# Softmax reciprocals of the first attention pass computed and fetched about one unit earlier

## The chip, the cores and the metric

The kernel runs on one core of one Trainium2 chip, in one launch. The metric is the device time of one execution in microseconds (us); lower is better. All data are 32-bit floats.

## The reference, cut to what matters

The input is 8 images of 32x32 positions with 512 channels. Two layers follow each other. Layer 0 is group norm, self-attention with 8 heads of 64 channels over the 1024 positions of an image, and a residual:

```
x_norm = group_norm(x)
q, k, v = split(x_norm @ w_qkv + b_qkv)          # 8 heads of 64
weight  = softmax((q * scale) @ (k * scale)^T)   # 1024 x 1024 for each head
out     = (weight @ v) @ w_out + b_out
x       = x + out
```

Layer 1 is a deformable attention: a layer norm and a projection, a depthwise 7x7 convolution with stride 2 that yields 256 sample points an image, keys and values from bilinear samples at these points, attention of all 1024 positions to the 256 samples, and a small MLP with residual. The change touches layer 0 alone, and in it the division by the softmax's sums.

## The kernel before, in words

The work of layer 0 (the first pass) is a row of 256 units, one after the other. A unit is one pair of heads and one tile of 128 queries of one image: 32 units an image (4 head pairs times 8 query tiles), 8 images. Four units in a row make a block of 512 queries for one head pair; there are 64 blocks, counted here from 0, so an image has eight.

The program of each engine is in the order in which the Python code issues it (`InOrder`). Work that belongs to other units is put in between by hand: `at(place, step)` files a step under a place on the axis of units, and `run_due(until)` issues all filed steps with a smaller place, in the order of their places. `push` for unit n issues, in this order:

- `scores`: 8 score matmuls on TensorE (two heads, 128 queries, 1024 keys), the negated row maximum on VectorE (`nmax`), the exponential on ScalarE (`e`), which also accumulates each row's sum in `sums`;
- all steps due before n + 0.8 (`before`);
- the transposes of `e` into `sq` on VectorE, in 32x32 squares;
- in odd units, `moved`: 16 copies that carry two units' squares from `sq` to `et`, which completes the transpose. They are issued on SyncE's queue (SP in the profile), which takes its instructions strictly in order;
- all steps due before n + 1 (`after`).

After an odd unit u, `attention_out` files the products with v under n = u + 3: `part` at n + 0.02 and n + 1.02, 16 matmuls each, which add up a block's output in the one PSUM tile `av` (`ps_av` has a single buffer). When u is the last unit of a block it also files the division:

- `share` (VectorE, then SP): the reciprocal of the block's sums into `rs`, a 32x32 transpose into `rsT`, and a DMA of 16 KB to a DRAM tile, `rs_d`;
- `spread` (SP): two DMAs that read `rs_d` back, each replicated over 64 partitions, into the tile `inv`. `inv` has one buffer in this pass (`n_inv` is 1), and these DMAs wait for the landing of `rs_d`;
- `scale` at n + 1.85 (VectorE): `attT` = `av` times `inv`. After it the next block may write `av`.

Other DMAs that SP carries in this pass, all in program order with those above: the results `mid` and `hat_d` of the image before, placed near the ends of units, and the operands `hat_x` of a convolution that is computed early beside the attention. Loads of x and of weights are issued by GpSimd (POOL), which also adds the convolution's taps and does part of the norms.

Of the kernel before, what the change touches and what calls it, by code (L numbers as in the profile page):

```python
# [240 lines left out]
def attention_then_deformable_attention(  # L241
# [115 lines left out]
    def at(place, step):  # L357
        due.append((place, len(due), step))
# [37 lines left out]
    with ExitStack() as l0:  # L396
# [54 lines left out]
        att = MovedAttention(nc, ident, ps_mm, ps_sc, ps_av, work, dram, 1)  # L451
# [181 lines left out]
        def attention_out(attT, hp, qt, n, et, sums, room):  # L633

            blk, t = divmod(qt, NQT)
            half = t // 2
            at(n + 0.02, lambda: att.part(et, room["v"], half, True))
            at(n + 1.02, lambda: att.part(et, room["v"], half, False))
            if half == 0:
                return  # L640

            share = {}

            def scale():
                t = attT[hp, blk] = work.tile([P, QB], F32, tag="attT", name="attT", bufs=NQB * NHP)
                att.scale(t, share["inv"])

            at(n - 1.1, lambda: att.share(sums))
            at(n - 0.1, lambda: share.update(inv=att.spread()))
            at(n + 1.85, scale)  # L650

        def last_places(n, t):
# [114 lines left out]
        for b in range(B):  # L767
# [20 lines left out]
            for hp in range(NHP):  # L788
                for qt in range(NT):
                    n = first + hp * NT + qt  # L790
                    if n % per == 0 and b > 0:
                        last, attT = attT, {}
                        out_steps(
                            b - 1, last,
                            [[n + p - 2.4, n + p - 1.4, n + p, int(n + p) + 0.85, n + p + 1.55]
                             for p in out_places],
                        )
                    t = qkv[b, hp]
                    et = att.push(
                        before=lambda n=n: run_due(n + 0.8),  # L800
                        after=lambda n=n: run_due(n + 1),
                        tiles=1,
                        at=qt % NQT,
                        q=t["q", qt // NQT][:, ts(qt % NQT, P)],
                        k=t["k"],
                    )
                    if et is not None:
                        attention_out(attT, hp, qt, n + 3, et, att.sums, t)
# [4 lines left out]
    with ExitStack() as l1:  # L813
# [56 lines left out]
        att = Attention(nc, ident, ps_mm, ps_sc, ps_av, work, dram, 2)  # L870
# [422 lines left out]
```

## Time and profile before

| | |
|---|---|
| three timed runs | 3562.83, 3573.17 and 3572.59 us; median 3572.59 us |
| profiled execution | 3563.64 us, of which the span of the core is 3561.9 us |
| first pass in the span | from the start to about 2240 us |
| busy over the span: PE / DVE / ACT / POOL | 3408.9 / 2527.3 / 1807.6 / 1538.3 us |
| `inv` reads: issues, time from issue to landing (min / median / max) | 256 in both passes, 3.3 / 4.4 / 9.1 us |

PE is the matmul engine TensorE, DVE is VectorE, ACT is ScalarE, SPq is SyncE's queue. Nearly all instructions go through one helper line, L54, so groups are told apart by the names of their tiles, output before input: `attT<-av,inv` is the step `scale`, `rsT<-rs` the transpose in `share`, `rs_d<-rsT` its DMA, `inv<-rs_d` the reads in `spread`, `et<-sq` the copies in `moved`. In a list of instructions the first column is the start and the second the duration, both in us; what stands in square brackets at the end of a row is the idle time of the engine just before it and what ended it. In a list of waits the three figures are the sum in us, how often, and the longest.

### The profile page before, as it was taken

What the parts mean: (1) busy time and instruction counts of PE and PEld (TensorE: products, weight loads), DVE (VectorE), ACT (ScalarE), POOL (GpSimd) and SP (SyncE); (2) the same over time, 40 slices, a digit from 0 to 9 for tenths busy, and PEclk for the clock granted to TensorE, in tenths of its full rate; (3) what the DMA queues carried; (4) which work ended last, traced back from release to release, by engine and by line L of the source; (5) the groups of instructions that cost most, each with busy time, mean ns of one, the idle gap of its engine ahead of it and who ended that gap; (6) DMA issues with size and microseconds to landing.
All of it is one profiled execution on the core that took longest, in us unless ns stands there. A gap on an engine that the chain in (4) does not pass through costs nothing.

```text
span 3561.9 us, 45200 instructions
## 1 busy us (share of the span) xinstructions
PE 3408.9 (96%) x14568; PEld 1686.4 (47%) x14568; DVE 2527.3 (71%) x3373; ACT 1807.6 (51%) x3919; POOL 1538.3 (43%) x1903
## 2 busy tenths in 40 slices
PE   7999999999999999999999998899998989899998
PEld 4444544554554454454454453444444444444443
DVE  4767778878878787788887876247767677665654
ACT  2343356566566566556566552135555455544442
POOL 1001216646735645654654653305444443542322
PEclk9999999999999999999999999899999999999999
DMA  4666657766766666666766766446556555555653
GB/s 141 167 162 174 195 157 193 209 164 177 218 160 172 201 175 186 196 184 168 205 180 167 205 175 187 155 136 201 190 174 196 167 191 171 187 195 188 223 185 126
DMA packets 446587, 641.64 MB, mean 180 GB/s; under 512 B 77104, under 2 KB 240944, under 8 KB 444304
## 3 DMA queue, kind: packets, MB, share of 16 engines
q1 hardware_dynamic: 415712, 536.67, 51.9%
q0 software_dynamic: 29488, 100.00, 9.4%
q8 instruction: 116, 1.90, 0.2%
q10 hardware_dynamic: 1152, 2.10, 0.2%
q14 instruction: 119, 0.97, 0.1%
HBM read 246.38 MB, written 123.73 MB: 104 GB/s over the span
## 4 chain that ended last, share of the span: by engine, by line
PE 75%; DVE 5%; SPq 5%; POOL 4%; ACT 4%; DMA 4%; issue 3%; POOLq 0%; DVEq 0%; ACTq 0%
PE mm L54 48%; PE sc L54 14%; PE av L54 13%; SPq L54 5%; ACT e L54 2%; DMA inv<-rs_d 1%; POOL chunk L54 1%; DVE sq L54 1%; DVE chunk L54 1%; POOL oa L54 1%; DVE nmax L54 1%; DMA et<-sq 1%; ACT L54 1%; POOL row L54 1%; DMA et<-sq_d 0%
## 5 line engine op out<-in xcount | busy, mean ns | idle before, releaser
L54 ACT ACTIVATE e<-sc,nmax 128x1024 f32<-128x1024 f32 (+1 forms) x1024 | 802.6, 797 | 627.9 <-DVE nmax L54 626.8
L54 DVE TENSOR_REDUCE nmax<-sc 128x1 f32<-128x1024 f32 (+1 forms) x640 | 750.6, 1214 | 351.3 <-PE sc L54 351.0
L54 DVE STREAM_TRANSPOSE sq<-e 128x1024 f32<-128x1024 f32 x640 | 764.6, 1225 | 253.2 <-ACT e L54 237.1
L54 POOL TENSOR_TENSOR oa<-part_x,oa 128x256 f32<-128x256 f32 x852 | 635.6, 746 | 590.4 <-ACT part_x L54 545.5
L54 ACT ACTIVATE part_x<-pad_x,dww_x 128x256 f32<-128x256 f32 x852 | 435.2, 541 | 241.8 <-POOL oa L54 239.4
L54 PE MATMUL sc<-k,q 64*128 64x512 f32 x2048 | 539.5, 619 | 18.8 <-ACT e L54 17.2
L54 PE MATMUL av<-et,v 128*64 128x256 f32 x4096 | 510.8, 393 | 33.4 <-DVE attT L54 18.5
L54 PE MATMUL mm<-xT,wqkv 128*128 128x512 f32 x1024 | 472.8, 606 | 3.1 <-issue 3.1
L54 PEld LDWEIGHTS av<-et,v 128*64 128x64 f32 x4096 | 277.1, 139 | 344.6 <-issue 156.7
L54 POOL TENSOR_TENSOR chunk<-parts,chunk 128x256 f32<-128x256 f32 x240 | 179.9, 750 | 388.7 <-ACT parts L54 375.2
L54 PEld LDWEIGHTS sc<-k,q 64*128 64x128 f32 x2048 | 187.3, 186 | 283.1 <-issue 190.6
L54 PEld LDWEIGHTS mm<-xT,wqkv 128*128 128x128 f32 x1024 | 187.9, 191 | 242.5 <-issue 236.8
L54 POOL TENSOR_TENSOR mv<-mv,minus_half 128x1 f32<-128x1 f32 x128 | 77.3, 604 | 509.5 <-DVE mv L54 508.2
L54 PEld LDWEIGHTS mm<-wqkv,xT 128*128 128x128 f32 x2048 | 234.7, 192 | 26.1 <-issue 26.1
L54 PE MATMUL mm<-wqkv,xT 128*128 128x128 f32 x2048 | 245.4, 278 | 0.0
L54 PE MATMUL mm<-wm,zT 128*128 128x512 f32 x512 | 238.4, 608 | 1.3 <-ACT zT L54 1.0
L54 PE MATMUL mm<-w,attT 128*128 128x512 f32 x512 | 235.5, 604 | 1.3 <-DVE attT L54 1.3
L54 PE MATMUL mm<-wo,attH 128*128 128x512 f32 x512 | 230.8, 593 | 0.4
L54 PE MATMUL mm<-hat_h,wqq 128*128 128x512 f32 x512 | 230.7, 593 | 0.0
L54 DVE SCALAR_TENSOR_TENSOR od<-pad_x,dww_x,od 128x256 f32<-128x256 f32 x276 | 216.9, 786 | 5.5
L54 ACT ACTIVATION_READ_ACCUMULATOR e<-sc,nmax 128x1 f32 x1024 | 209.4, 204 | 0.0
L54 PE MATMUL mm<-w,hat_x 128*128 128x512 f32 x384 | 172.7, 600 | 0.0
(163 smaller groups left out, 3565.3 us busy)
## 6 DMA issues: line engine op xcount, KB each, us to landing
et<-sq SPq DMA_DIRECT2D x2048, 128.0 KB, 2.8
sq_d<-sq SPq DMA_DIRECT2D x128, 512.0 KB, 4.4
et<-sq_d SPq DMA_DIRECT2D x128, 512.0 KB, 4.2
inv<-rs_d SPq DMA_DIRECT2D x256, 128.0 KB, 4.4
hat_h<-hat_d SPq DMA_DIRECT2D x16, 1024.0 KB, 7.9
xr<-mid SPq DMA_DIRECT2D x64, 256.0 KB, 5.4
x<-in_x_dram POOLq DMA_DIRECT2D x60, 256.0 KB, 4.0
out_dram<-res POOLq DMA_DIRECT2D x60, 256.0 KB, 3.3
```

Of the source, the lines that this page charges most:

```text
L54: return self.tc.keep_in_program_order(op(*args, **kwargs))
```

## The change

Two places change by hand, both in `attention_out`. With u for the last unit of the block (n = u + 3), `share` moves from u + 1.9 to u + 1.1 and `spread` from u + 2.9 to u + 1.9.

```
-            at(n - 1.1, lambda: att.share(sums))
-            at(n - 0.1, lambda: share.update(inv=att.spread()))
+            at(n - 1.9, lambda: att.share(sums))
+            at(n - 1.1, lambda: share.update(inv=att.spread()))
             at(n + 1.85, scale)
```

In the order of issue this means: `share` runs in the `before` part of unit u + 1 (ahead of that unit's transposes) where it ran in its `after` part; `spread` runs in the `after` part of unit u + 1, so ahead of the 16 copies of unit u + 2, where it ran behind them. The place of `scale`, the amount of work and all tiles stay as they were.

## The prediction

> **What bounds the kernel now.** I read the page's busy line first, then the list of waits, then the instructions around one wait, then windows with the granted clock.
>
> ```profile
> PE 3408.9 (96%) x14568; PEld 1686.4 (47%) x14568; DVE 2527.3 (71%) x3373; ACT 1807.6 (51%) x3919; POOL 1538.3 (43%) x1903
> ...
> PE 75%; DVE 5%; SPq 5%; POOL 4%; ACT 4%; DMA 4%; issue 3%; POOLq 0%; DVEq 0%; ACTq 0%
> ```
>
> TensorE carries the time. The second line is the chain that ended last: 14% of it lies on SPq, DMA and VectorE together, where PE stood waiting. A change that removes no matmul can gain only what PE waits. The list of waits says where:
>
> ```profile
> DVE attT L54 <- DMA inv<-rs_d: 66.4, 38, 5.4
> ...
> PE av L54 <- DVE attT L54: 18.5, 9, 3.3
> ...
> PE av L54 <- DMA et<-sq: 14.0, 3, 8.2
> ```
>
> VectorE's `scale` waited 38 times of 64 for the broadcast reciprocals. Nine times this reached PE, since the next block's first product may not write `av` before `scale` has read it: 18.5 us. The third row is put down to the copies, but is mostly the same wait. At 102.94 us the group of copies had landed at 99.83, and `attT` ended only at 102.9; the other two are taken up below. The wait at block 13, engine by engine (SP, DVE, PE):
>
> ```profile
> 490.88 0.33 SPq L54 DMA_DIRECT2D rs_d<-rsT  x1
> 497.21 11.16 SPq L54 DMA_DIRECT2D et<-sq  x16
> 508.42 1.27 SPq L54 DMA_DIRECT2D inv<-rs_d  x2
> ...
> 507.46 2.37 DVE L54 STREAM_TRANSPOSE sq<-e 128x1024 f32<-128x1024 f32 x2 [1.23 <-ACT e L54]
> 513.99 0.69 DVE L54 TENSOR_TENSOR attT<-av,inv 128x512 f32<-128x512 f32 x1 [4.16 <-DMA inv<-rs_d]
> ...
> 509.42 1.99 PE L54 MATMUL sc<-k,q 64*128 64x512 f32 x8
> 514.74 3.38 PE L54 MATMUL av<-et,v 128*64 128x256 f32 x16 [3.33 <-DVE attT L54]
> ```
>
> The reads of `inv` stood behind 16 copies in SP's order, though `rs_d` had landed 16 us earlier (492.29). They landed at 513.87; VectorE idled 4.16 us, PE 3.33 us. Of those 3.33 us the copies explain nothing: they had landed at 510.50. And the same 16 matmuls, 1.95 us elsewhere, took 3.38 us. The windows show why (first figure PE's busy time; the clock stands after POOL's):
>
> ```profile
> 511.40:514.70 3.30, 0.01 (x1) 0.00 (x0) 0.71 (x2) 0.00 (x0) 0.76 (x2) 0.93 0.87 216
> 514.70:517.70 3.00, 2.96 (x14) 1.71 (x16) 2.96 (x4) 0.94 (x1) 0.00 (x0) 0.50 0.95 308
> ```
>
> After the idle stretch the clock is at half for 3 us (back at 1.00 after 517.7): half of that is lost too.
>
> **Part 1: the waits that go.** `spread` now precedes the 16 copies. Its new landing is estimated for each block as the end of unit u's copies, plus that block's own landing times of `rs_d` and `inv`: it comes 6 to 25 us before `scale` could start, in every block but the last. (Block 63 stays: its `share` and `spread` are issued behind the same last copies as before.) So each `scale` runs when VectorE reaches it, and PE next waits for the later of its own work and the copies. The nine gaps are .36, .23, 3.33, 2.50, 3.04, 2.43, 3.29, 2.80 and .49 us, six of them the sixth block of an image (blocks 13 to 53). In those six the copies landed 0.9 to 1.7 us before PE would need them, so all 18.5 us go. The 2.7 us of block 0 go. At 2168.60 (block 61, gap 3.0) the copies landed only at 2165.90, and part 2 delays them by 0.8: 1.9 us go. At 2194.82 (block 62, gap 8.2) the copies landed at 2191.63: 3.1 us go and 5 us stay. Sum 18.5 + 2.7 + 1.9 + 3.1 = 26.2 us.
>
> The clock comes on top. The records show half clock after five of these gaps, at 514, 1068, 1347, 1900 and 2169 us, for 2.9, 5.9, 3.4, 2.9 and 3.4 us of matmuls: half of 18.5 is 9.3 us. Here the Trainium skill speaks otherwise: "TensorE: Matmul & The Clock Gate", Part 1, has the array fall to half clock after an idle window of about 3.4 us. The gaps here, 2.4 to 3.3 us, are shorter; by the rule none would cost clock, and the sum would be 26.2. The trace has half clock after five and none after those of 2.5 us at 791.83 and 3.29 us at 1624.95. I take the trace's 9.3. The dip at 2190 us I leave, as 5 us of its gap stay.
>
> I take off 2.5 us for the short gaps of the first image and of 2108, where PE elsewhere waits for exponentials (17 gaps, 17.2 us, `sc<-k,q` on `e`) and may give the time back. Net gain: 26.2 + 9.3 - 2.5 = 33.0 us.
>
> **Part 2: what moves on SP's queue.** Per block one `rs_d` issue (0.3 to 0.8 us) and two `inv` issues (1.27 us), no more than before. `rs_d` now issues right behind unit u's copies, ahead of `mid` and `hat_d` placed late in unit u + 1; these go later by the half microsecond of that issue, and wait for results of VectorE and POOL anyway. The new cost is that SP stands at `inv` until `rs_d` has landed, with the next 16 copies behind it.
>
> ```profile
> 612.89 14.06 SPq L54 DMA_DIRECT2D et<-sq  x16
> 627.05 0.54 SPq L54 DMA_DIRECT2D hat_d<-hat  x1
> 627.68 0.53 SPq L54 DMA_DIRECT2D mid<-xr  x1
> 628.30 0.58 SPq L54 DMA_DIRECT2D hat_d<-hat  x1
> 628.97 0.76 SPq L54 DMA_DIRECT2D rs_d<-rsT  x1
> 630.34 13.03 SPq L54 DMA_DIRECT2D et<-sq  x16
> ```
>
> This is the tightest kind: 3.4 us from one group of copies to the next. With `rs_d` at 627.05, its own landing of 3.6 us and 1.3 us for `inv`, the next copies start at about 632.0, 1.6 us late. They had landed 7.1 us before PE used them, and no `inv` follows them now. Over the blocks this room is 2.1 to 13 us, and `rs_d` landed in 1.4 to 7.6 us in this pass (median 2.4). Here a rule speaks against the change: "DMA: Bandwidth & Descriptors", Anatomy of one DMA, says that a wait on a semaphore is sat out by the issuing sequencer and that most of a fixed 2 us is the receipt from the target memory. With 2 us, 7 of 63 groups of copies start late, with the 3.6 us measured in this busy place 17, by up to about 3 us, and in both cases none later than PE needs it. I take 3.6 and 0 us.
>
> A second hold is none: `inv` has one buffer, but the previous `scale` ends about 13 us before the new issue (613.6 against about 630 above). POOL's queue gets nothing new and nothing on it is passed.
>
> **Part 3: VectorE.** Reciprocal 0.20 and transpose 0.21 us come 64 times, before and after. They now stand between `nmax` and `sq`, which delays unit u + 1's squares by 0.4 us; their copies go only with unit u + 2. The next `nmax` waits behind the same sum of work. Taken as 0; if the cover is gone in a quarter of the 17 gaps on `e`, 1.6 us, and if it were gone in all blocks, 64 times 0.41 = 26 us. The 66 us of VectorE's idle time at `scale` that vanish feed no other row: where PE did not wait, the next `nmax` waited for scores.
>
> **Rivals.**
> (a) *The next thing is late.* PE's wait at `attT` becomes one on the copies, which in the sixth blocks land only 0.9 to 1.7 us ahead. If they land 2 us later, the seven gaps keep about 1 us each and perhaps the clock dips: gain 33 - 7 - 7 = 19 us, 3554 us. Against it: in these blocks SP idles 6 us before that group, so it is not pushed.
> (b) *Nothing.* The reads land earlier but the matmuls after them wait for exponentials, or `inv` is held by something the trace does not show: 3562 to 3580 us. Against it: the gaps end within 0.1 us of `attT`.
> (c) *Slower: SP blocks on the landing of `rs_d`.* If behind 16 copies in flight `rs_d` needs L us, PE's new stall, summed over the groups' measured room, is 0 up to 3.65, 2.4 us at L = 5, 15.6 at 7, 41.9 at 9, 70.6 at 10. Against a gain of 33 it decides from about 8.6 us; at 9.5 it gives 3572.6 + 56 - 33 = 3596 us. For it: landings of 7.2 and 7.6 us exist. Against it: four fifths are below 3.7.
> That the change does not do what it says I exclude: the steps are filed when `push` of unit u has returned, and both places lie in unit u + 1.
>
> **The numbers.** The sum is made on the profiled execution: 3563.6 - 33.0 = 3530.6 us. The median of the runs is 9 us above that execution; from the median it is 3572.6 - 33.0 = 3539.6, and I give 3539. Chances: forecast 0.70, (a) 0.14, (b) 0.08, (c) 0.08. About 0.3%, 11 us, is what a measurement here can tell from no change. Faster by more 0.84, within 0.08, slower 0.08. The range reaches down to the profiled base with some 10 us of secondary gain (3521) and up through (a), to 3562.
>
> **What would show it.** Right: no row of `attT` waiting for `inv` over a few us in sum, PE's waits for `attT` near 0, the sixth blocks at full clock, `inv` issued ahead of each even group of copies and SP waiting there for `rs_d` 1 to 4 us. Wrong: new rows of `av` waiting for `et<-sq` well over 14 us, or landings of `rs_d` above 8 us. If the waits vanish and the time does not fall, look at `sc<-k,q` on `e`.

## The result and the profile after

| | before | after |
|---|---|---|
| timed runs (before: the three above and one more) | 3555.2 to 3573.2 us, median 3567.7 (4 runs) | 3522.9 to 3528.6 us, median 3526.4 (4 runs) |
| profiled execution / its span | 3563.64 / 3561.9 us | 3522.86 / 3521.2 us |
| the first pass ends (its last output product, `mm<-w,attT`, starts) at | 2234.1 us | 2199.2 us |

The changed kernel is faster: the ratio is 0.9888, with a 95% interval of 0.9858 to 0.9919, so 1.1% or about 41 us. The forecast was 3539 us in a range of 3521 to 3562.

The busy line and the chain of the page after:

```profile
PE 3388.6 (96%) x14568; PEld 1679.5 (48%) x14568; DVE 2534.7 (72%) x3373; ACT 1809.8 (51%) x3919; POOL 1536.3 (44%) x1903
...
PE 81%; POOL 4%; ACT 4%; DVE 4%; issue 3%; DMA 2%; SPq 2%; POOLq 0%; ACTq 0%; DVEq 0%
```

PE's share of the chain rose from 75% to 81%; SPq, DMA and VectorE gave up what it gained. PE is also busy 20 us less for the same matmuls, since more of them run at full clock: in these two profiles the granted clock is at half for 159 us in sum before and for 116 after, and half of the difference is 21 us. The list of waits after, for VectorE, PE and SP (us in sum, times, longest):

```profile
DVE attT L54 <- DMA inv<-rs_d: 2.1, 1, 2.1
...
PE av L54 <- DMA et<-sq: 13.0, 4, 6.5
...
SPq L54 <- DMA rs_d<-rsT: 108.3, 57, 6.4
```

`scale` waits for its reciprocals once (the last block), where it waited 38 times; PE has no row of `av` behind `attT` left. What came instead is on SP: it stands 57 times for the landing of `rs_d`, 108 us in sum. Block 13 again, by SP, DVE and PE:

```profile
485.21 0.53 SPq L54 DMA_DIRECT2D rs_d<-rsT  x1
487.48 1.27 SPq L54 DMA_DIRECT2D inv<-rs_d  x2
493.15 10.86 SPq L54 DMA_DIRECT2D et<-sq  x16
...
505.69 0.65 DVE L54 TENSOR_TENSOR attT<-av,inv 128x512 f32<-128x512 f32 x1
...
505.35 1.99 PE L54 MATMUL sc<-k,q 64*128 64x512 f32 x8
507.27 1.95 PE L54 MATMUL av<-et,v 128*64 128x256 f32 x16
```

The reads now issue 6 us ahead of the 16 copies, not behind them. `attT` starts when the transposes ahead of it on VectorE end, and the product follows the scores without a gap and takes 1.95 us, not 3.38. The window of that product has the clock at 1.00:

```profile
507.20:510.20 3.00, 3.00 (x21) 1.63 (x20) 2.97 (x5) 1.33 (x3) 1.01 (x2) 1.00 0.82 220
```

In the tightest kind of block (around 630 us before), SP's queue reads:

```profile
617.20 0.53 SPq L54 DMA_DIRECT2D hat_d<-hat  x1
617.83 0.43 SPq L54 DMA_DIRECT2D mid<-xr  x1
618.35 0.86 SPq L54 DMA_DIRECT2D rs_d<-rsT  x1
...
621.75 1.28 SPq L54 DMA_DIRECT2D inv<-rs_d  x2
623.13 13.48 SPq L54 DMA_DIRECT2D et<-sq  x16
```

The squares of the last group were ready at 621.04, so this group starts 2.1 us late (1.6 was estimated), and PE, which uses it at 643.3, does not notice. A row of `hat_d` and one of `mid` still stand ahead of `rs_d`: it passes only some of them, not all as the forecast had it.

**Where the time went.** The lead of the changed kernel is the start of the same product before minus after, in the first profiles of the two kernels. A block's gap at `attT` lies ahead of the next block's first product and is counted with the block whose `attT` it is.

| stage of the first pass | lead at its end, us | gained in it |
|---|---|---|
| up to block 12 | 3.8 | 3.8 |
| six sixth blocks (13 to 53), each with its clock stretch | | 5.1 + 2.9 + 6.3 + 4.7 + 3.7 + 4.6 = 27.3 |
| all other blocks up to 60 | 33.7 | 2.6 |
| blocks 61 to 63, up to the last output product | 34.8 | 1.1 |
| from there to the end of the program | 40.8 | 5.9 |

### The profile page after: what moved, and what is told of

It is laid out like the page before. It is cut to its first block, busy times and chain, and to the rows that moved or that the text cites. A ratio compares the mean times of both kernels' runs of the same rounds, so it can differ in the third digit from the quotient of the medians.

```text
span 3521.2 us, 45344 instructions
## 1 busy us (share of the span) xinstructions
PE 3388.6 (96%) x14568; PEld 1679.5 (48%) x14568; DVE 2534.7 (72%) x3373; ACT 1809.8 (51%) x3919; POOL 1536.3 (44%) x1903
## 4 chain that ended last, share of the span: by engine, by line
PE 81%; POOL 4%; ACT 4%; DVE 4%; issue 3%; DMA 2%; SPq 2%; POOLq 0%; ACTq 0%; DVEq 0%
PE mm L54 51%; PE sc L54 16%; PE av L54 15%; ACT e L54 2%; SPq L54 2%; POOL chunk L54 1%; POOL row L54 1%; DVE chunk L54 1%; ACT L54 1%; DVE nmax L54 1%; POOL oa L54 0%; DMA et<-sq_d 0%; DMA sq_d<-sq 0%; POOL rows L54 0%; POOL hat L54 0%
## 5 line engine op out<-in xcount | busy, mean ns | idle before, releaser
L54 PE MATMUL sc<-k,q 64*128 64x512 f32 x2048 | 536.6, 619 | 17.1 <-ACT e L54 15.4
L54 PE MATMUL av<-et,v 128*64 128x256 f32 x4096 | 503.5, 388 | 13.9 <-DMA et<-sq 13.0
L54 DVE SCALAR_TENSOR_TENSOR od<-pad_x,dww_x,od 128x256 f32<-128x256 f32 x276 | 226.4, 820 | 5.5
## 6 DMA issues: line engine op xcount, KB each, us to landing
et<-sq SPq DMA_DIRECT2D x2048, 128.0 KB
inv<-rs_d SPq DMA_DIRECT2D x256, 128.0 KB
```

What stands on the lines that cost most here:

```text
L54: return self.tc.keep_in_program_order(op(*args, **kwargs))
```

## The experiments

Two theories were to be told apart first. *Order on SP*: the time was lost because the reads stood behind 16 copies in SP's order. *VectorE's order*: the gain comes from the reciprocal moving away from in front of the next `nmax`. All edits are to the two places, or to the queue, of the first pass.

**The reciprocal alone moved.**

```
+            at(n - 1.9, lambda: att.share(sums))
             at(n - 0.1, lambda: share.update(inv=att.spread()))
```

> Only the reciprocal and its DMA move (u + 1.1); the broadcast reads stay behind the 16 copies at u + 2.9. Theory (the reads' place in SP's order is what cost): the 38 waits of attT for inv stay near 66 us, PE's gaps at attT stay near 18 us, and the time is that of before within 0.3% (3557 to 3578). Rival (VectorE's order, the reciprocal out of the way of the next nmax): the gain comes here, 3525 to 3540.

Measured: 3568.7 us, ratio to before 0.9997 (0.9983 to 1.0011). Its waits of VectorE, and of PE:

```profile
DVE attT L54 <- DMA inv<-rs_d: 69.1, 34, 7.5
...
PE av L54 <- DVE attT L54: 19.5, 8, 3.6
```

All the waits are still there. The VectorE theory falls.

**The reads alone moved.**

```
             at(n - 1.1, lambda: att.share(sums))
+            at(n - 1.05, lambda: share.update(inv=att.spread()))
```

> Only the reads move: the reciprocal stays at u + 1.9 and the reads follow it at u + 1.95, ahead of the copies of u + 2. Theory: the waits of attT for inv vanish and most of the gain comes (3525 to 3545), but SP stands longer for the landing of rs_d, 130 to 200 us in sum instead of 108, and some groups of copies come later than with the full change, which may cost it 0 to 10 us. Rival (VectorE's order): no gain, 3560 to 3578.

Measured: 3531.6 us, ratio 0.9891 (0.9872 to 0.9909), within the interval of the full change. Waits of VectorE and SP:

```profile
DVE attT L54 <- DMA inv<-rs_d: 1.9, 1, 1.9
...
SPq L54 <- DMA rs_d<-rsT: 148.0, 64, 5.5
```

The place of the reads is the whole change, as far as can be measured. Moving the reciprocal as well spares SP 40 us of standing (148 against 108), and that is worth nothing that these runs resolve.

**The change in the sixth block of each image alone, and in all other blocks alone.**

```
+            early = (hp, blk) == (2, 1)     # the complement: !=
+            at(n - (1.9 if early else 1.1), lambda: att.share(sums))
+            at(n - (1.1 if early else 0.1), lambda: share.update(inv=att.spread()))
```

> The full change in the sixth block of each image alone (8 of 64 blocks). Theory (six of the gaps and their half-clock stretches are there): 25 to 30 us of the 41, so 3538 to 3546. Rival (a gain spread over all 64 blocks, or the clock's luck): an eighth, about 5 us, 3560 to 3568.

Measured: 3539.5 us, ratio 0.9915 (0.9897 to 0.9933).

> The complement of the run with the sixth blocks alone: the full change in the 56 other blocks, the old places in the sixth block of each image. Theory (the gain is local to the gaps): the six gaps and their half clock stay, so 5 to 14 us of gain remain, 3554 to 3564, and the two partial gains add up to about the whole. Rival (the two parts share one cause, either alone brings most): 3530 to 3545.

Measured: 3558.8 us, ratio 0.9974 (0.9964 to 0.9984). So 8 of the 64 blocks bring 0.85% and the 56 others 0.26%; together 1.11%, against 1.12% for the whole. VectorE's wait rows of the two show how little an idle sum says (first the sixth blocks alone, then the rest alone):

```profile
DVE attT L54 <- DMA inv<-rs_d: 40.8, 28, 4.9
```

```profile
DVE attT L54 <- DMA inv<-rs_d: 32.3, 8, 7.2
```

With 41 us of waits left the kernel has most of the gain; with 32 us left it has a quarter. Of the eight waits left in the second kernel, seven are those of the sixth blocks of images 1 to 7 (images, like blocks, are counted from 0), and after each of them PE idles, for 2.0 to 4.8 us.

**Another queue for the reads, both places as before.**

```
-            self.nc.sync.dma_start(
+            self.nc.gpsimd.dma_start(      # spread, first pass
```

> Both places as before the change; only the queue of the two reads is changed, from SP to POOL, in the first pass. Theory (being behind the copies in SP's order made the reads late): attT no longer waits for inv (under 10 us), SP never stands for rs_d, and the time is that of the changed kernel or some us less, 3518 to 3535. Rival (the moment of issue in the program matters, or POOL becomes late with 128 more DMAs of about 0.6 us each): no gain or slower than before, 3560 to 3600.

Measured: 3536.9 us, ratio 0.9903 (0.9886 to 0.9921). With the old places, and nothing changed but the queue, the gain is there: standing behind the copies was the cause, not the moment in the program. The bound of 3535 that was expected was missed by 2 us. POOL's waits and VectorE's show what this queue cost:

```profile
POOL inv L54 <- DMA rs_d<-rsT: 82.0, 21, 26.0
...
DVE attT L54 <- DMA inv<-rs_d: 12.4, 1, 12.4
```

POOL stood 82 us for `rs_d`. In the last block its reads, behind the norms of the last rows, came so late that `attT` idled 12.4 us and PE 12.3.

**Is SP's standing free? The write of `rs_d` by POOL, on top of the full change.**

```
-        nc.sync.dma_start(self.share_d, turned)
+        nc.gpsimd.dma_start(self.share_d, turned)     # share, first pass
```

> The full change, with the 16 KB write of rs_d issued by POOL in the first pass, so it need not queue behind unit u's copies. Takes away SP's standing at the reads: the wait of SPq for rs_d falls from 108 us to under 30. Theory (that standing is covered by the room ahead of PE's use, all but at the end of image 7): no change that can be measured, 3518 to 3530. Rival (the standing costs PE, the gain would have been larger without it): 10 us or more below the changed kernel, under 3516.

Measured: 3527.7 us, ratio 0.9896 (0.9877 to 0.9914). SP's row:

```profile
SPq L54 <- DMA rs_d<-rsT: 24.2, 18, 3.6
```

84 us of standing are gone and the time is the same, so SP's standing is covered as far as this run can tell: POOL has 64 more DMAs to issue here, and what they may have taken back was not separated. The run with the reads alone agrees from the other side, with 40 us more of standing and the same time. At the end of image 7 the gap of block 61 shrank from 4.0 to 1.2 us, but others of 5.0 and 3.7 us stood close by.

**How long may SP stand? One and two more copies of `rs_d` from DRAM to DRAM in front of the reads.**

```
+        for i in range(1):     # 2 in the second kernel
+            hop = self.dram.tile([P, SQ], F32, tag=f"hop{i}", name=f"hop{i}", bufs=3)
+            self.nc.sync.dma_start(hop, self.share_d)
+            self.share_d = hop
```

> The full change with one more DRAM to DRAM copy of rs_d in front of the reads, on SP, so that SP stands for two landings in a row (L about 5 to 6 us instead of 2.7, and 0.5 us more to issue). By the prediction's table of room: 2 to 10 us lost against the changed kernel, 3527 to 3537. Rival (room is larger than the table says, as groups follow one another): nothing lost, 3522 to 3528.

Measured: 3531.3 us, ratio to before 0.9913 (0.9887 to 0.9940).

> Two such copies in front of the reads: SP stands for three landings in a row, L about 8 to 9 us. By the prediction's table 27 to 45 us lost, so about the time of before, 3550 to 3575, with new rows of av waiting for et<-sq of 20 us and more. Rival (SP's queue catches up, PE never sees it): under 3535.

Measured: 3575.8 us, ratio to before 1.0022 (1.0011 to 1.0034). The time from the issue of `rs_d` to the first read is 2.7 us in the median of the changed kernel, 5.3 us with one copy, 7.1 with two (8 to 9 had been expected); the first pass ends at 2199.2, 2206.7 and 2243.2 us. PE's row of the second kernel, which had 13.0 us in 4 waits without the copies:

```profile
PE av L54 <- DMA et<-sq: 42.9, 16, 9.8
```

So the rival of the forecast that ends on the other side exists: with the reads in the better place and a hold of 7 us, the kernel is slower than before, by 0.2%. The hold of the real change is 4.4 us away from that in the median.

**Both kernels profiled a second time**, for the 5.9 us gained behind the first pass.

> The changed kernel unaltered, for a second profile. In the first one the stretch between the last output product of pass one and the first attH took 124.3 us against 131.0 before, with 23.9 us at half clock against 41.0. Theory (that stretch varies with the clock's phase and is no effect of the change): it comes anywhere from 119 to 132 us, following the half-clock time, while the first pass again ends near 2199 us. Rival (the change shortens that stretch): 124 us again within a microsecond.

> The kernel before, unaltered, for a second profile. Theory: the first pass ends at 2230 to 2242 us with gaps at attT in the sixth blocks again, and the stretch after it takes anywhere from 119 to 132 us. Rival (the stretch is fixed by the order of the first pass): 131 us again.

| | time, us | first pass ends | from there to the first `attH` of the second pass | of it at half clock |
|---|---|---|---|---|
| before | 3563.64 | 2234.1 | 131.0 | 41.0 |
| before, again | 3565.32 | 2237.8 | 128.0 | 27.3 |
| after | 3522.86 | 2199.2 | 124.3 | 23.9 |
| after, again | 3530.49 | 2200.2 | 130.9 | 34.1 |

The end of the first pass comes again within 4 us and 1 us. The stretch behind it goes back to 130.9 us for the changed kernel, so its 6.7 us are no effect of the change. The half-clock time in it differs by 10 to 14 us between executions of one kernel. Between the second profiles the lead is 1.1 us up to block 12, the six sixth blocks give 32.2 us (all six gaps were followed by half clock there), the first pass as a whole 37.6.

## Why the prediction was right, point by point

**The mechanism** is as forecast, and shown by three runs from different sides: the reads moved alone, the queue changed alone, and the reciprocal moved alone, which does nothing. The rows named as its signs came (no `attT` behind `inv`, reads ahead of each even group, SP standing for `rs_d`, the sixth blocks at full clock).

**The nine gaps and their clock.** 17.4 us of gaps and 7.6 us of half clock were entered for the six sixth blocks, 25.0. They gave 27.3: 17.8 in the gaps, 7.4 in the products after them, and 2.1 that were not entered, in score products of the same blocks ahead of the gap. To count the clock from the trace was right: by the rule of the Trainium skill ("TensorE: Matmul & The Clock Gate", Part 1), by which gaps this short cost no clock, these blocks would have given 17.4. The run with sixth blocks alone gave 0.85% of 3568, about 30 us, with the two other such blocks (5 and 61) in it. Rival (a) did not come in these six blocks: PE waits for copies in none of them, in either profile of the changed kernel.

**The end of image 7** is the step that failed: "1.9 us go" at block 61 with 1.7 of clock, and 3.1 at block 62. Of these 6.7 us the first profiles have 1.5 up to the last group's product, the second ones 0.9. SP and PE after, at block 61:

```profile
2119.04 1.26 SPq L54 DMA_DIRECT2D inv<-rs_d  x2
2120.40 7.80 SPq L54 DMA_DIRECT2D et<-sq  x8
...
2135.91 2.55 PE L54 MATMUL av<-et,v 128*64 128x256 f32 x16 [4.01 <-DMA et<-sq]
```

PE's gap grew from 3.0 to 4.0 us (from 4.9 to 5.5 in the second profiles), with `et<-sq` as its releaser. The group was entered as 0.8 us late. It began 1.7 us after its squares were ready (2120.40 against 2118.69), and then its seventh and eighth copies stood 2.0 and 0.2 us for the landing of the two reads: in the trace each of these copies waits for the DMA eight places ahead of it in SP's order. Six loads of rows from POOL were under way, and the first read took 7.8 us to land. The second profile of the changed kernel has such a wait of 2.9 us at the same place, the run with the reads alone one of 2.1. It was not in the forecast at all: reads ahead of the copies do not only pass first, the copies also wait for them when they land slowly. The old order is not free of it: copies stood there behind slow copies for 0.9 us in the second profile of before and for 1.9 us in the run that left the sixth blocks as they were. So it is not shown how much of the longer gap is due to the reads.

**The start.** For the gaps up to block 12 3.3 us were entered; the lead there is 3.8 us in the first profiles and 1.1 in the second. Block 0, whose 2.7 us were to go, gave 0.8 of them in the first profile: PE waited 1.9 us there for the copies themselves, as rival (a) has it. In the second profile that gap is gone. Much of the rest is not the change's: between 90 and 103 us the clock is at half for 6.8 us in the first profile before and for 3.4 in the one after, and the second profile of before is 4.0 us ahead of the first by 309 us of time, without the change, since a half-clock stretch at 234 us is missing there.

**The 2.5 us taken off** for time given back were not given back. The waits of scores for `e` near the starts of images 2 to 7 fell from 1.27, 1.39, 1.30, 1.23, 0.91 and 1.60 us to 0.94, 0.91, 0.94, 0.92, 0.93 and 1.05, 2.0 us in sum. The reads bring this: in the run with the reads alone these waits are 0.90 to 0.93 us, with the reciprocal alone 0.93 to 1.73. By which path was not traced.

**The hold on SP** was put at up to 3 us for 17 groups and 0 us of time. The standing is there (108 us), and taking 84 us of it away moved nothing that can be measured: right, but for block 61. The 2 us that the forecast took from the Trainium skill ("DMA: Bandwidth & Descriptors", Anatomy of one DMA) are given there for DMAs that GpSimd issues; on SP the landing of `rs_d` had a median of 2.4 us before.

The price curve of rival (c) was too flat. It has about 4 us at L = 5.3 and 16 at 7.1; the copies in front of the reads cost 7.5 and 44 us of the first pass. PE's waits for copies grew by 6.0 and 29.9 us, and the half-clock time behind the first 40 us from 20.5 to 23.9 and 51.2 us; half of that growth is 1.7 and 15.4 us, so the two together make up the loss to within 2 us. The curve left the clock out. It also let each group start from its old time; that a late group makes the next one late is the likely reason for the longer waits, but was not traced. The curve decides from about 7 us, not from 8.6. (The "about 13 us" from the end of the previous `scale` to the new issue are 16 by the two figures beside them; nothing rests on it.)

**VectorE's part** at 0 is right: share alone, 0.9997.

**The sum.** 33.0 us against 34.8 in the first pass of the first profiles and 37.6 of the second. That 33.0 and 34.8 lie so close is in part luck: the end of image 7 fell short by 5.6 us, and the sixth blocks, the waits for `e` and the start made it up. On the profiled execution the forecast was 3530.6; the two profiled executions of the changed kernel took 3522.9 and 3530.5. Between 3539.6 and the median of 3526.4 lie 13 us. About 5 are the base: the three runs of before had a median of 3572.6, four had 3567.7, and 43 later ones 3568.2. The other 8 are a gain of 41 us, not 33. Of the 41, 36 lie in the first pass by the mean of the two profiles of each kernel, and 5 are not settled: the stretch behind it moves by as much between executions of one kernel.

## What to carry to other kernels

On a queue that takes its instructions in order, the place of a small DMA among bulk copies decides when it lands: find the slot where its data are ready and the queue idles, and look at what it then holds up, both by waiting for its own operand and by landing slowly ahead of others. Rank waits by whether they reach the engine that bounds the kernel, not by their sum: 8 of 64 blocks held three quarters of this gain. Count the clock lost after an idle stretch with the stretch itself, and check a change's edge by making its worst case longer, as the two extra copies did.

## What the runs showed of the hardware

Idle stretches of PE of 2.3 to 4.1 us were followed by half clock, but not each time: of the six sixth blocks, with gaps of 2.4 to 3.3 us in the first profile of before, four were followed by half clock, and in its second profile (2.3 to 4.1 us) all six. The clock came down to half for 3.4 or 6.8 us at a time. Gaps of nearly equal length (3.29 and 3.33 us, 2.50 and 2.43) cost nothing more or about 1.5 us, and one of 3.04 us cost 2.9; one execution cannot tell such a cost to better than that.

From the issue of a 16 KB write to DRAM to that of the first read of it on the same queue, 2.1 to 7.4 us passed (median 2.7); a further copy from DRAM to DRAM in the row added 2.7 us to the median, and a second one 1.8 us.
